# One gathered tile in 64 moved from GpSimd's queue to SyncE's, in a relational graph layer on one core

## The chip, the cores and the metric

The kernel runs on one core of a Trainium2 chip. The time is the device time of one launch, in microseconds. Three runs of the kernel before took 2102.25, 2105.05 and 2107.07 us, with a median of 2105.05 us. The profiled execution is a fourth run and has its own time, which is given below. The engines are named as in the profile: PE is TensorE (PEld its weight loads), DVE is VectorE, ACT is ScalarE, POOL is GpSimd and SP is SyncE. An engine's name with a q behind it (SPq, DVEq) is its sequencer, which issues DMAs, waits for semaphores and loads registers.

## The reference

There are 12,500 nodes with 256 features, and 212,500 edges sorted by destination. Each edge has one of 8 types, and each node's last edge is its loop to itself.

```python
h = jnp.maximum(_layernorm(x, axis=-1), 0.0)
hx = jnp.einsum('ni,rio->rno', h, weight)          # 8 products per node
msg = hx[edge_type, src]
agg = jax.ops.segment_sum(msg, dst, num_segments=num_nodes)
out = x + agg * 0.5 ** 0.5 + h_bias + (h @ loop_weight) * 0.5 ** 0.5
```

## The kernel before

**What is summed where.** The kernel does not form `hx`. It sums the rows of `h` by destination node and edge type first, and multiplies by the 8 weights afterwards. The sums stand transposed in SBUF in `acc`, a ring of 6 slots of 128 nodes.

**Edges.** They are cut into 802 units of 256 edges (in the first 128 units) or 267 edges (after those). A self loop is taken out of a unit's list and handled by node, so what is left fits 256 places. A unit is two tiles of 128 edges, and there are 1603 tiles in all. Units are prepared in 7 blocks of up to 128. For each block `load_indices` (line 304) loads source, destination and type of its edges into `nat_s`, `nat_d` and `nat_t`, some 45 small VectorE steps turn them into row numbers `gidx`, columns `col` and ring offsets, and `blocks_ahead` spreads these steps over the tiles before the block is needed, three steps in every second tile. The last block is not full. There the unused places are filled first: `nat_s` and `nat_t` by a VectorE memset, `nat_d` by a GpSimd iota (line 317). Only then are its rows loaded.

**One tile.** `gather` (line 671) lets GpSimd fetch 128 rows of 256 numbers, chosen by one column of `gidx`, with one indirect DMA (line 683) into `msg`. Until the normalized table `h32` has been written, the rows come from `x` and are normalized in place. After that they come from `h32`. `edge_sums` (line 713) multiplies the rows with a one-hot matrix `oh` in four matmuls (line 723), and `add_sums` (line 731) lets VectorE add the result of a pair of tiles to the ring, at an offset that VectorE's sequencer holds in a register. `load_offsets` (line 704) fills 16 such registers at a time with one load.

**The loop.** It stands in an order written out by hand (line 1030): in step `t` the gather of tile `t + AHEAD` (58) is issued, then the one-hots, the sums of tile `t`, background steps, and pieces of the work on finished groups of 128 nodes. The pool of `msg` has `MSGS // PAIR` = 31 buffers of two tiles. A gather into a buffer waits until the matmuls that read it last are done, so gathers can lead the matmuls by at most about 60 tiles. Each engine takes its own instructions strictly in this order.

**Groups.** When all edges of a group are in, 18 products (line 883) are queued between the following tiles. Three tiles behind them comes `finish` (line 891): VectorE adds `x`, SyncE stores four groups at once (line 900), and the slot is cleared for a later group by `begin` (line 765), which fills it with that group's self loops in eight VectorE instructions (line 773). For these, the loops' types are needed by node. Every fourth group, `finish` calls `mark` (line 780, VectorE), `find_types` (line 793: small TensorE products at line 800 that read what `mark` wrote, then VectorE, then ScalarE) and, three tiles later, `spread_types` (line 822). The order in `finish` is `begin`, `mark`, `find_types`, so in TensorE's list the products of line 800 stand directly behind work on VectorE that is still to be done.

**SyncE** issues all plain transfers, in the order of the loop: the block loads (lines 322 and 325), the loads of `h` and `x` for four groups (line 839) and the stores (line 900). The compiler hands these transfers eight semaphores in turn, and a transfer waits until the one issued eight before it has landed.

Of the kernel before, what the change touches and what calls it, by code (L numbers as in the profile page):

```python
# [11 lines left out]
I32 = mybir.dt.int32  # L12
AF = mybir.ActivationFunctionType
ALU = mybir.AluOpType
# [4 lines left out]
DVE = mybir.EngineType.DVE  # L19

P = 128
EPS = 1e-5
ALPHA = 0.5

# [4 lines left out]
EDGES = 267  # L29
# [9 lines left out]
CLEARED = 3  # L39
RING = GROUP * SLOTS  # L40

MSGS = 62
AHEAD = 58


# [7 lines left out]
REST = 3  # L53
# [2 lines left out]

ROWS = 6
FIRST = 4

LATE = 8  # L60

# [148 lines left out]
def kernel(  # L210
# [11 lines left out]
    nc = tc.nc  # L222
    N, D = x.shape
# [7 lines left out]
    NT = plan.NT  # L231
    U = PAIR * P
    NU = plan.NU
    EU = plan.EU
# [30 lines left out]
    def place_of(t):  # L265
        u, i = divmod(t, PAIR)
        return u // P, i, u % P


    with ExitStack() as main:  # L270
# [25 lines left out]

        outs = [ps_o.tile([P, 2, D], F32, name=f"po{i}") for i in range(2)]
        msg, oh, offsets, kind = {}, {}, {}, {}
        firsts, stops, loops, marked, typed, gidx, col = {}, {}, {}, {}, {}, {}, {}
        added, zeroed = {}, {}  # L300
        state = {"h32": None}
# [2 lines left out]
        def load_indices(b):  # L304

            rows_ = min(P, NU - b * P)
            last = b == NB - 1
            full = rows_ - last
            size = EDGES if b else U
            e0 = P * U + (b - 1) * P * EDGES if b else 0  # L310
            nat = {}
            for name, a, more in (("s", src, 0), ("d", dst, 1 if b else 0), ("t", etype, 0)):
                n = ep.tile([P, EDGES + 1], I32, name=f"nat_{name}")
                if last:

                    if more:
                        nc.gpsimd.iota(
                            n, pattern=[[2, EDGES + 1]], base=N - 2 * EU, channel_multiplier=0)
                    else:
                        nc.vector.memset(n, -1 if name == "d" else 0)  # L320
                if full:
                    nc.sync.dma_start(n[:full, : size + more], bass.AP(
                        tensor=a.tensor, offset=a.offset + e0, ap=[[size, full], [1, size + more]]))
                if last:
                    nc.sync.dma_start(
                        n[full : full + 1, :EU], a[E - EU : E].rearrange("(p q) -> p q", p=1))
                nat[name] = n
            return nat

        def turned(got, cols, to):  # L330

            def turn():
                pt = ps_d.tile([P, 512], F32, tag="pt", name="ptr")
                for i in range(PAIR):
                    half = slice(i * P, (i + 1) * P)
                    nc.tensor.transpose(pt[:, half], got[cols][:, half], ident)
                nc.vector.tensor_copy(to(), pt[:, :U])

            return [turn]
# [5 lines left out]
        def compacted(got, bit, bits):  # L345

            def step(k):
                m = work_tile(got, "moves", 5, I32)
                nc.vector.tensor_single_scalar(m, packed, 1 << (bit + k), op=ALU.bitwise_and)  # L349
                nc.vector.copy_predicated(  # L350
                    packed[:, : EDGES - (1 << k)], m[:, 1 << k :], packed[:, 1 << k :])

            return [lambda k=k: step(k) for k in range(bits)]

        def sources(b, got):


            if b == 0:
                def copy():
                    nc.vector.tensor_copy(work_tile(got, "sf", 2)[:, :U], got["s"][:, :U])  # L360

                return [copy, *turned(
                    got, "sf", lambda: gidx.setdefault(b, idx.tile([P, U], I32, name="gidx")))]

            def rises():
                nc.vector.tensor_tensor(  # L366
                    work_tile(got, "rise", 0), got["d"][:, 1:], got["d"][:, :EDGES], op=ALU.subtract)

            def stays():
                nc.vector.tensor_scalar(  # L370
                    work_tile(got, "stay", 1), got["rise"], 0.0, None, op0=ALU.is_equal)
                firsts[b] = small.tile([P, 1], F32, name="firsts")
                nc.vector.tensor_copy(firsts[b], got["d"][:, 0:1])

            def shifts():
                nc.vector.scalar_tensor_tensor(
                    work_tile(got, "code", 2), got["d"][:, :EDGES], firsts[b], got["stay"],
                    op0=ALU.subtract, op1=ALU.mult)

            def codes():  # L380
                nc.vector.scalar_tensor_tensor(
                    got["code"], got["code"], float(R), got["t"][:, :EDGES], op0=ALU.mult, op1=ALU.add)

            def packs():
                nc.vector.scalar_tensor_tensor(
                    packed, got["s"][:, :EDGES], float(1 << (TB + SB)), got["code"],
                    op0=ALU.mult, op1=ALU.add)

            def unpacks():
                nc.vector.tensor_single_scalar(  # L390
                    work_tile(got, "from", 5, I32)[:, :U], packed[:, :U], TB + SB,
                    op=ALU.logical_shift_right)
                nc.vector.tensor_scalar(
                    work_tile(got, "sf", 2)[:, :U], got["from"][:, :U], 0.0, float(N - 1),
                    op0=ALU.max, op1=ALU.min)
                nc.vector.tensor_single_scalar(
                    work_tile(got, "rest", 3, I32)[:, :U], packed[:, :U], (1 << (TB + SB)) - 1,
                    op=ALU.bitwise_and)

            return [rises, stays, shifts, codes, packs, *compacted(got, TB, SB), unpacks,  # L400
                    *turned(got, "sf", lambda: gidx.setdefault(b, idx.tile([P, U], I32, name="gidx")))]

        def last_edges(b, got):

# [266 lines left out]
        def gather(t):  # L671
            if t % PAIR == 0:
                both = msgs.tile([P, PAIR, D], F32, name="msg")
                for i in range(PAIR):
                    msg[t + i] = both[:, i, :]
            if t % QUAD:
                kind[t] = kind[t - 1]
            else:
                kind[t] = "h" if state["h32"] is not None and t >= state["h32"] + LATE else "x"
            table = {"h": h32, "x": x}[kind[t]]  # L680
            b, i, u = place_of(t)
            at = i * P + u
            nc.gpsimd.indirect_dma_start(  # L683
                out=msg[t], out_offset=None, in_=table[:, :],
                in_offset=bass.IndirectOffsetOnAxis(ap=gidx[b][:, at : at + 1], axis=0))

        def onehots(t):

# [133 lines left out]
        def spread_types(q):  # L822

            pt = ps_d.tile([P, 512], F32, tag="pt", name="ptt")
            nc.tensor.matmul(pt, ones_b, marked.pop(q), start=True, stop=True)
            typed[q] = types.tile([P, XG * GROUP], BF16, name="types")
            nc.scalar.activation(typed[q], pt, AF.Copy)

        got = {}
# [40 lines left out]
        def group_work(g):  # L870
# [20 lines left out]
            def finish():  # L891
                q, k = divmod(g, XG)
                rows_ = got["x", q]
                nc.vector.tensor_add(rows_[:n, k, :], rows_[:n, k, :], outs[g % 2][:n, 1, :])  # L894
                nc.vector.tensor_add(rows_[:n, k, :], rows_[:n, k, :], got["out", g][:n])  # L895
                if XG * (q + 1) >= plan.NG:
                    nc.sync.dma_start(out[d0 : d0 + n], rows_[:n, k, :])
                elif k == XG - 1:
                    first = plan.starts[XG * q]
                    nc.sync.dma_start(  # L900
                        out[first : d0 + n].rearrange("(k p) d -> p k d", p=P), rows_)
                b = g + SLOTS
                q, k = divmod(b, XG)
                if b < plan.NG:
                    if q < plan.typed:
                        clear(b)
                    else:
                        begin(b)
                if q + 1 >= plan.typed and XG * (q + 1) < plan.NG:
                    if k == XG // 4:  # L910
                        load_groups("h", h32, q + 1)
                    if k == XG - 2:
                        mark(q + 1)
                    if k == XG - 1:
                        find_types(q + 1)
                        done["late"].append((done["tile"] + REST, lambda: spread_types(q + 1)))

            def last():
                done["late"].append((done["tile"] + REST, finish))
# [8 lines left out]
        with tc.manual_schedule():  # L928
# [101 lines left out]
            for t in range(NT):  # L1030
                done["tile"] = t
                if t + AHEAD < NT:
                    gather(t + AHEAD)
                blocks_ahead(t)
                for f in after:
                    f()
# [92 lines left out]
```

## Time and profile before

| | |
|---|---|
| median of three runs | 2105.05 us |
| profiled execution: its time, its span | 2107.2 us, 2105.2 us |
| PE busy | 1789.1 us (85%) |
| DVE busy | 1327.7 us (63%) |
| POOL busy | 1523.2 us (72%) |
| gathers (line 683) | 1603 in all: 96 from `x`, 1507 from `h32` |
| granted PE clock, mean | 0.924 |
| DMA | 281.17 MB, mean 134 GB/s |

The span is the profiled stretch from the first instruction to the last. The busy time of an engine is what its instructions took; waits and the sequencer's own work (register loads, DMA issues) are not in it. So an engine that is 72% busy can still be the one that never rests, when there is a fixed gap behind each of its instructions. In the lists of waits, the name behind the arrow is what ended the wait; "issue" means that nothing in the profile ended it.

### The profile page before, as it was taken

Reading aid. Unit: us, or ns where it says so; the run is one execution under the profiler, and the core shown is the slowest. Engines: PE = TensorE matmul, PEld = TensorE weight load, DVE = VectorE, ACT = ScalarE, POOL = GpSimd, SP = SyncE. Lnnn points to the kernel's source line nnn. Section 1 sums busy time; section 2 is a strip of 40 time slices with the busy share of each in tenths; the row PEclk is TensorE's granted clock in tenths of the full one; section 3 lists DMA queues with packets and bytes.
Section 4 is the critical chain, followed back from the end, with each engine's and each line's share of the span. In section 5 each row is a group of like instructions: output and inputs, shape, how many; then the busy total and the mean of one; then the engine's idle time right before and its main releaser. Section 6 shows DMA issues by size and latency. Waiting matters only on the chain.

```text
span 2105.2 us, 29382 instructions
## 1 busy us (share of the span) xinstructions
PE 1789.1 (85%) x10411; PEld 1644.1 (78%) x10411; DVE 1327.7 (63%) x3274; ACT 218.5 (10%) x470; POOL 1523.2 (72%) x1630
## 2 busy tenths in 40 slices
PE   2468999998999998999988998988998860799998
PEld 2357998888898888888877887877888750698897
DVE  7869666668666687665686655577665520856652
ACT  7854100000000000000000000000000000000000
POOL 7767777777777777777777777777777777677750
PEclk8578999998999999999999999999999985899999
DMA  8963443443444344344344344343443433343430
GB/s 297 373 208 103 145 136 106 136 144 106 135 136 135 105 142 135 106 135 136 106 143 131 109 135 135 107 143 106 135 135 106 135 106 106 117 127 105 130 91 15
DMA packets 146904, 281.17 MB, mean 134 GB/s; under 512 B 28125, under 2 KB 95460, under 8 KB 146756
## 3 DMA queue, kind: packets, MB, share of 16 engines
q0 software_dynamic: 76944, 210.21, 34.2%
q1 hardware_dynamic: 69812, 69.05, 10.2%
q8 instruction: 85, 1.39, 0.3%
q14 instruction: 63, 0.52, 0.1%
HBM read 253.55 MB, written 25.60 MB: 133 GB/s over the span
## 4 chain that ended last, share of the span: by engine, by line
PE 67%; DVE 13%; issue 6%; DMA 6%; POOL 4%; ACT 2%; SPq 0%; DVEq 0%; ACTq 0%; POOLq 0%
PE ps L723 34%; PE po L883 31%; DMA msg<-h,gidx 4%; POOL msg L683 4%; DVE acc L773 3%; DVE acc L735 2%; DVE moves L349 2%; DVE fixed L350 2%; DMA h<-xt 1%; ACT xt L645 1%; DVE oh L696 1%; PE pst L759 1%; DMA w<-in_L_gnn_weight_dram 1%; DVE n_stats L633 0%; PE ptt L800 0%
## 5 line engine op out<-in xcount | busy, mean ns | idle before, releaser
L683 POOL DMA_INDIRECT msg<-h,gidx x1507 | 1430.0, 949 | 481.7 <-issue 396.3
L723 PE MATMUL ps<-oh,msg 128*128 128x176 f32 (+1 forms) x6412 | 1146.2, 310 | 187.5 <-DVE acc L735 76.6
L723 PEld LDWEIGHTS ps<-oh,msg 128*128 128x128 f32 x6412 | 1056.2, 198 | 290.1 <-issue 100.9
L883 PE MATMUL po<-w,acc 128*128 128x256 f32 x3136 | 892.7, 387 | 0.0
L696 DVE TENSOR_TENSOR oh<-fixed,cols 128x704 f32<-128x704 f32 x402 | 356.0, 886 | 356.2 <-PE ps L723 349.3
L883 PEld LDWEIGHTS po<-w,acc 128*128 128x128 f32 x3136 | 547.4, 195 | 25.3
L735 DVE TENSOR_TENSOR acc<-acc,ps 128x352 f32 x802 | 412.9, 515 | 180.9 <-PE ps L723 171.9
L773 DVE SCALAR_TENSOR_TENSOR acc<-types,pst 128x256 f32<-128x256 bf16 (+1 forms) x688 | 234.8, 414 | 74.5 <-ACT self_t L762 73.0
L762 ACT ACTIVATE self_t<-pst 128x256 f32<-128x256 f32 x98 | 37.5, 383 | 1524.5 <-PE pst L759 1524.5
L883 PE MATMUL po<-wl,self_t 128*128 128x256 f32 x392 | 121.2, 438 | 3.9 <-ACT self_t L762 2.4
L683 POOL DMA_INDIRECT msg<-in_x_dram,gidx x96 | 90.9, 947 | 31.1 <-issue 26.2
L883 PEld LDWEIGHTS po<-wl,self_t 128*128 128x128 f32 x392 | 75.7, 214 | 11.9 <-ACT self_t L762 2.8
L800 PE MATMUL ptt<-loops,mark 128*128 128x24 bf16 x216 | 9.3, 179 | 80.8 <-DVE acc L773 80.8
L800 PEld LDWEIGHTS <-mark 128*128 128x128 bf16 x216 | 7.3, 101 | 85.7 <-DVE acc L773 85.7
L366 DVE TENSOR_TENSOR rise<-nat_d 128x267 f32<-128x267 int32 x6 | 2.6, 432 | 79.0 <-DMA nat_d<-in_dst_dram 79.0
L645 ACT ACTIVATE xt<-xt,n_shift,n_rstd 128x256 f32<-128x256 f32 x98 | 50.9, 589 | 11.0 <-DVE n_shift L642 11.0
L645 ACT ACTIVATE msg<-msg,e_shift,e_rstd 128x256 f32<-128x256 f32 x96 | 49.6, 589 | 8.5 <-DVE e_shift L642 8.1
L894 DVE TENSOR_TENSOR xr<-xr,po 128x256 f32<-128x256 f32 x98 | 40.4, 412 | 7.4 <-PE po L883 7.4
L895 DVE TENSOR_TENSOR xr<-xr,po 128x256 f32<-128x256 f32 x98 | 41.2, 421 | 3.4
L818 ACT ACTIVATE diagonal<-ident,kinds 128x128 bf16<-128x128 f32 x88 | 28.1, 390 | 113.8 <-DVE kinds L815 113.8
L759 PE MATMUL pst<-ident,hr 128*128 128x128 f32 x196 | 37.7, 274 | 0.4 <-DVE offs L586 0.2
L349 DVE TENSOR_SCALAR moves<-fixed 128x267 int32<-128x267 int32 x84 | 36.4, 433 | 1.7
(200 smaller groups left out, 402.3 us busy)
## 6 DMA issues: line engine op xcount, KB each, us to landing
msg<-h,gidx POOLq DMA_INDIRECT x1507, 2.8
xt<-in_x_dram SPq DMA_DIRECT2D x24, 512.0 KB, 6.4
h<-xt SPq DMA_DIRECT2D x24, 512.0 KB
xr<-in_x_dram SPq DMA_DIRECT2D x24, 512.0 KB, 7.1
hr<-h SPq DMA_DIRECT2D x24, 512.0 KB, 6.3
out_dram<-xr SPq DMA_DIRECT2D x24, 512.0 KB, 4.0
w<-in_L_gnn_weight_dram SPq DMA_DIRECT2D x2, 1024.0 KB, 8.3
msg<-in_x_dram,gidx POOLq DMA_INDIRECT x96, 5.8
```

Source lines behind the costliest of these rows:

```text
L349: nc.vector.tensor_single_scalar(m, packed, 1 << (bit + k), op=ALU.bitwise_and)
L350: nc.vector.copy_predicated(packed[:, : EDGES - (1 << k)], m[:, 1 << k :], packed[:, 1 << k :])
L645: nc.scalar.activation(rows_[j], rows_[j], AF.Relu, bias=shift[:n, j : j + 1], scale=rstd[:n, j : j + 1])
L683: nc.gpsimd.indirect_dma_start(out=msg[t], out_offset=None, in_=table[:, :], in_offset=bass.IndirectOffsetOnAxis(ap=gidx[b][:, at : at + 1 ...
L696: nc.vector.tensor_tensor(o[:, k : k + v, :i, :], iota_f.unsqueeze(1).unsqueeze(1).to_broadcast([P, v, i, C]), of.unsqueeze(3).to_broadcas ...
L723: nc.tensor.matmul(ps[:, c, from_ : from_ + width], m[:, c * P : (c + 1) * P], o[:, :width], start=(i == 0 and c == 0), stop=(end and c == ...
L735: i = nc.vector.tensor_tensor(a, a, ps, op=ALU.add)
L759: nc.tensor.transpose(pst[:, c, :n], rows_[:n, c * P : (c + 1) * P], ident[:n, :n])
L773: i = nc.vector.scalar_tensor_tensor(acc[:, :, r, s0 : s0 + n], of, float(r + 1), pst[:, :, :n], op0=ALU.is_equal, op1=ALU.mult)
L883: i = nc.tensor.matmul(got["out", g][:n], lhs, rhs, start=(r == R and c == 0), stop=(r == R - 1 and c == KC - 1))
L894: nc.vector.tensor_add(rows_[:n, k, :], rows_[:n, k, :], outs[g % 2][:n, 1, :])
L895: nc.vector.tensor_add(rows_[:n, k, :], rows_[:n, k, :], got["out", g][:n])
```

## The change

There are four edits.

- **Rows fetched by SyncE.** In blocks 1 to 6, a tile whose number is 63 modulo 64 is no longer gathered by GpSimd (if it lies within the loop's reach and `h32` is in use). Its 128 rows are fetched by 128 single-row DMAs on SyncE's queue. The row numbers come from a new tile `single` (an integer copy of the second half of the block's row numbers, not transposed): a register load brings 16 of them to SyncE, and 16 DMAs follow, each from an address computed from its register. `fetch(FETCH)` puts three of these items (a load or a DMA) into each step of the loop. There are 20 such tiles, 319 to 1535, so 2560 DMAs, 160 register loads and 2560 address computations are added to SyncE's list, and 20 gathers leave GpSimd's.
- **`MSGS` 60 instead of 62**: one buffer of two tiles less, `AHEAD` unchanged.
- **The last block's places** of `nat_d` are filled by VectorE from `line`, not by GpSimd's iota.
- **`find_types` three tiles later**, and `spread_types` three tiles after that.

```diff
@@ constants
-MSGS = 62
+MSGS = 60
 AHEAD = 58
+SINGLE = 64
+FETCH = 3
+SOURCES = 16
@@ load_indices
                     if more:
-                        nc.gpsimd.iota(
-                            n, pattern=[[2, EDGES + 1]], base=N - 2 * EU, channel_multiplier=0)
+                        nc.vector.tensor_scalar(
+                            n, line[:, : EDGES + 1], 2.0, float(N - 2 * EU), op0=ALU.mult, op1=ALU.add)
@@ new: the last step of sources(b, got)
+        def kept_sources(b, got):
+            def keep():
+                single[b] = idx.tile([P, P], I32, name="single")
+                nc.vector.tensor_copy(single[b], got["sf"][:, P:U])
+            return [] if b == 0 else [keep]
@@ gather
             b, i, u = place_of(t)
+            if b and i and kind[t] == "h" and t % SINGLE == SINGLE - 1 and t + AHEAD < NT:
+                for r in range(0, P, SOURCES):
+                    fetches.append(lambda r=r: load_sources(t, r))
+                return
             at = i * P + u
             nc.gpsimd.indirect_dma_start(
@@ new
+        def load_sources(t, r0):
+            b, _, u = place_of(t)
+            _, vals = nc.values_load_multi_w_load_instructions(
+                single[b][u : u + 1, r0 : r0 + SOURCES], engines=[SP], min_val=0, max_val=N - 1,
+                skip_runtime_bounds_check_because="clamped to the table where they are computed")
+            for i, v in reversed(list(enumerate(vals))):
+                fetches.insert(0, lambda i=i, v=v: nc.sync.dma_start(
+                    msg[t][r0 + i : r0 + i + 1, :], h32[bass.ds(v, 1), :]))
+        def fetch(n):
+            for _ in range(min(n, len(fetches))):
+                fetches.pop(0)()
@@ finish
                     if k == XG - 1:
-                        find_types(q + 1)
-                        done["late"].append((done["tile"] + REST, lambda: spread_types(q + 1)))
+                        done["late"].append((done["tile"] + REST, lambda: find_types(q + 1)))
+                        done["late"].append((done["tile"] + 2 * REST, lambda: spread_types(q + 1)))
@@ loop
                 if t + AHEAD < NT:
                     gather(t + AHEAD)
+                fetch(FETCH)
                 blocks_ahead(t)
```

More of the change, by code (lines that the diff above doesn't have):

```diff
@@ L21 @@
 P = 128
+SP = mybir.EngineType.SP
 EPS = 1e-5
@@ L298 @@
         msg, oh, offsets, kind = {}, {}, {}, {}
+        single, fetches = {}, []
         firsts, stops, loops, marked, typed, gidx, col = {}, {}, {}, {}, {}, {}, {}
@@ L400, in sources @@
             return [rises, stays, shifts, codes, packs, *compacted(got, TB, SB), unpacks,
-                    *turned(got, "sf", lambda: gidx.setdefault(b, idx.tile([P, U], I32, name="gidx")))]
+                    *turned(got, "sf", lambda: gidx.setdefault(b, idx.tile([P, U], I32, name="gidx"))),
+                    *kept_sources(b, got)]
         def last_edges(b, got):
```

## The prediction, made before the changed kernel ran

> **What bounds the kernel now.** I read the costliest groups first, then the waits, then windows by stage. The chain of waits is read last: it ends in TensorE, and it hides what set the pace.
>
> ```profile
> PE 67%; DVE 13%; issue 6%; DMA 6%; POOL 4%; ACT 2%; SPq 0%; DVEq 0%; ACTq 0%; POOLq 0%
> L683 POOL DMA_INDIRECT msg<-h,gidx x1507 | 1430.0, 949 | 481.7 <-issue 396.3
> ...
> POOL msg L683 <- issue: 306.8, 1007, 0.3
> POOL msg L683 <- PE ps L723: 31.4, 103, 0.3
> ...
> PE ps L723 <- DMA msg<-h,gidx: 25.7, 37, 2.0
> ```
>
> The second line is the key. A gather takes 0.949 us, and most of the idle time before gathers is "issue", which nothing ended. The two POOL waits are those between 225 and 1710 us: none is longer than 0.3 us. So GpSimd starts a gather every 1.25 us (0.95 and a fixed 0.30) and is full at 72% busy. The last line is TensorE from 975 to 1710 us: it waits for gathered rows 37 times, so the rows set the pace there. The windows (start and end, length, busy time and number, for TensorE its weight loads beside it, then granted clock, DMA share, GB/s) count gathers in the first three lines and tile matmuls, four a tile, in the last two:
>
> ```profile
> 125.00:225.00 100.00, 68.55 (x73) 0.85 0.42 125
> 225.00:975.00 750.00, 567.84 (x599) 0.96 0.44 128
> 975.00:1710.00 735.00, 556.49 (x587) 0.96 0.43 126
> ...
> 225.00:975.00 750.00, 451.14 (x2612) 422.85 (x2610) 0.96 0.44 128
> 975.00:1710.00 735.00, 418.36 (x2350) 378.62 (x2351) 0.96 0.43 126
> ```
>
> GpSimd holds 750/599 = 735/587 = 1.252 us per gather. TensorE does 653 tiles in the first long window, 1.149 us each, and eats its backlog (58 tiles at 225 us, 4 at 975 us by counting both). After that it goes at GpSimd's pace. From 125 to 225 us there are 73 gathers where 80 would fit: the `msg` buffers are full there.
>
> Then something else happens:
>
> ```profile
> DVE rise L366 <- DMA nat_d<-in_dst_dram: 79.0, 2, 74.4
> PE ptt L800 <- DVE acc L773: 80.8, 21, 7.8
> PE ps L723 <- DVE acc L735: 76.6, 11, 66.6
> ...
> 1782.61 0.37 POOL L317 IOTA nat_d<- 128x268 int32 x1
> ...
> 1784.86 0.44 DVE L366 TENSOR_TENSOR rise<-nat_d 128x267 f32<-128x267 int32 x1 [74.36 <-DMA nat_d<-in_dst_dram]
> ...
> 1787.02 1.51 PE L723 MATMUL ps<-oh,msg 128*128 128x176 f32 x4 [66.64 <-DVE acc L735]
> ```
>
> The iota of the last block takes 0.37 us, but in GpSimd's list it stands behind the 58 gathers that the loop issues ahead. VectorE waits 74.4 us for the load behind it, and TensorE 66.6 us for VectorE. GpSimd goes on gathering, fills its buffers, and is then held by TensorE. At its last gather (2035.8 us) TensorE still has some 40 tiles to do, so the stall comes back as a late end: the span is 2105.2 us.
>
> **Part by part.**
>
> *Iota moved to VectorE.* It removes the 74.4 us wait, and with it TensorE's 66.6 us. Late next is GpSimd's own pace: TensorE stays 4 tiles behind the gathers to the end. The fill itself costs VectorE about 0.44 us (L366 above, nearly the same shape). VectorE now waits for its loads, which stand in SyncE's list behind 11 rows of a fetch: 11 x 0.41 (below) + 6 loads x 0.35 + landing 1.8 (1783.00, the load's issue, to 1784.86) is about 8 us instead of 74, and the chain of gathers does not see it.
>
> *20 gathers leave GpSimd.* 20 x 1.252 = 25 us off the chain that sets the pace.
>
> *One `msg` pair less.* Where the buffers are full (before 225 us), gathers lead by two tiles less: 2 x 1.25 = 2.5 us later from there on.
>
> *Type products three tiles later.* They take up to 80.8 us of waits from TensorE. TensorE is ahead of its rows or catching up with them, so I count nothing. What hides it is the gather pace; with that cover gone it would be worth up to 80 us. The residual wait is bounded by today's 3.8 us per call; the latest user of the types comes 10 tiles after `spread_types`.
>
> *The sum for GpSimd's chain.* By 224.7 us 168 gathers have started (96 from `x`, 72 from `h32`). Of 1603, 1435 are left; plus 2, less 20, is 1417. Tile 1600 is the third from the end: 224.7 + 1414 x 1.252 = 1995, and 2.8 us to landing (page, part 6) gives 1998. The end is the same program as now:
>
> ```profile
> 2080.66 0.76 PE L723 MATMUL ps<-oh,msg 128*128 128x176 f32 x4
> ```
>
> That is tile 1600, 24.5 us before the span's end (the queued products of the last groups). 1998 + 24.5 = 2022.5 us of span. The execution is 2.0 us longer than its span, and the median of the runs lies 2.15 us below the profiled one: 2022.
>
> *The 2560 row fetches.* This is the price that no row shows. Per tile, SyncE needs 128 x (address, DMA, two gaps) and 8 loads of 16 registers. The nearest rows:
>
> ```profile
> L325 SPq DMA_DIRECT2D nat_d<-in_dst_dram x1: 233/233/233, 1783.4 to 1783.4; - x1
> L325 SPq DMA_DIRECT2D nat_t<-in_edge_type_dram x1: 246/246/246, 1784.0 to 1784.0; - x1
> ...
> L735 DVEq FUSED_REGOPS  x802: 69/69/69, 39.6 to 2086.3; - x161
> L602 SPq FUSED_REGOPS  x1: 181/181/181, 1831.7 to 1831.7; - x1
> L707 DVEq TENSOR_LOAD <-offs x51: 539/1100/3781, 12.2 to 2042.5; - x51
> ```
>
> L325 loads a single row: 0.246 us of SyncE, from a fixed address; a register's address may cost more. The address is between 0.07 (VectorE's sequencer, also multiplications for an address) and 0.18 (SyncE's own, but comparisons). I take 0.07, the same kind of work. The gaps are 0.045 each (SyncE's loads at 1710.24 and 1710.60, the first taking 0.32). So a row is 0.41 us (0.52 with the other end), 128 rows 52 us, the loads 8 x 1.15 = 9.2: 61 us. Between the rows stand a store, a load of `h` and one of `x` (0.38, 0.50, 1.07 by their medians, 2.1 with gaps), and as a transfer waits for the one eight before it, the 512 KB loads (6.3 and 7.1 us to landing) hold the rows for up to 3.0 and 3.8 us. The fetch of a tile takes 61 to 70 us. The time it has: its first row waits for the matmuls 60 tiles earlier, and 60 tiles at the new pace (1.252 x 63/64 = 1.232) are 74 us, less 2.1 for landing (the shortest load on the page is an estimate for it): 72. It fits, with 2 to 11 us to spare. I add 6 us for loads that collide and rows that come late: **2028 us**.
>
> [...]
>
> **The rivals.**
>
> *SyncE becomes the bound (slower).* If a fetch takes F > 72 us, TensorE waits for its last row, and gathers, at most 60 tiles ahead, wait with it: each of some 18 to 20 cycles is longer by F - 72. Back at today's time when the excess is (2105 - 2022)/19 = 4.4 us, that is F = 76 us or a row of about 0.47 us. With the upper address price (0.52 us) F is 76 to 85, and the time 2022 + 19 x (4 to 13) = 2098 to 2270; middle 2165. For it: the margin is thin, and the register address is unpriced. Against: the one-row DMAs are short, and SyncE has little else to do, a store and two loads per 65 tiles.
>
> *SyncE late by little.* Rows of 0.44 to 0.47 us: 2040 to 2095.
>
> *TensorE becomes the bound.* At 1.149 us per tile from tile 110 (225 us) it would do tile 1600 at 1937 us, 60 before the rows. It would have to lose 4% first; if the wait of the last block came back in full at the same place, the end would be about 2022 + 58 = 2080.
>
> *The removed gathers or the iota bring nothing.* Without the 20 gathers' gain the sum is 2047. GpSimd's row shows no slack in which it could vanish.
>
> **How the numbers follow.** Chances: the forecast 0.52; SyncE late by little 0.07; SyncE the bound and slower 0.37; about equal 0.02; the two others 0.02. Forecast's own range: 2015 to 2045 (chain sum less 7 for a better start, plus 23 for some late cycles). The range for 8 in 10 goes up into SyncE's case, to 2200 (rows of 0.52 us in the middle of their stalls), and down to 2012. A measurement of this kernel tells 0.2% from no change (4 us; its three runs lie within 0.23%). Faster 0.60, same 0.02, slower 0.38.
>
> **What would show it.** Right: no wait of 66 us in TensorE; gathers 1.25 us apart to the end, the last near 1998 us; SyncE's rows at most 0.43 us apart; no wait of TensorE for rows fetched by SyncE above 1 or 2 us. L800's waits shrink without moving the end. Wrong: TensorE waiting every 64 tiles for `msg` landing from SyncE, and gathers waiting for TensorE behind it; then the row's price was the failed step. A start of a fetch held by a store's wait would be another.

## The result and the profile after

The changed kernel takes 2031.35 us (median of six runs) where the kernel before takes 2105.78 us: a ratio of 0.9641, with a 95% interval of 0.9627 to 0.9654. The forecast was 2028 us. One of the six executions took 3686.84 us; it has no profile, the ratio leaves it out (without it the median is 2030.82 us), and nothing here explains it. The profiled execution is 2030.82 us, its span 2029.1 us.

The page of the changed kernel, the chain that ended last by engine and the gathers' group:

```profile
PE 33%; SPq 24%; issue 14%; DMA 11%; DVE 11%; POOL 4%; ACT 2%; DVEq 0%; ACTq 0%; POOLq 0%
...
L703 POOL DMA_INDIRECT msg<-h,gidx x1487 | 1411.4, 949 | 467.8 <-issue 387.2
```

20 gathers fewer, at the same 949 ns. The chain now names SyncE with 24%, though its rows turn out below to cost almost nothing; in the equally fast run without the moved types (below) it names SyncE with 10%. So a share in this view is no price: where two causes end nearly together, it names the later one.

Windows of the changed kernel, gathers (start and end, length, busy time and number, granted clock, DMA share, GB/s):

```profile
125.00:225.00 100.00, 64.67 (x69) 0.83 0.41 121
225.00:975.00 750.00, 567.78 (x599) 0.97 0.45 130
975.00:1710.00 735.00, 556.34 (x587) 0.97 0.44 129
1710.00:2000.00 290.00, 219.62 (x232) 0.99 0.42 121
```

GpSimd starts as many gathers per stretch as before (599 and 587), and goes on like that to the end: 290/232 = 1.25 us. That is the pace of the whole kernel. Only the first window is worse, 69 gathers where the kernel before has 73. From 225 us on nothing holds GpSimd: of all its waits there, none is longer than the fixed 0.3 us (in all, times, longest, us):

```profile
POOL msg L703 <- issue: 365.7, 1200, 0.3
POOL msg L703 <- PE ps L757: 40.2, 132, 0.3
```

Windows of the changed kernel, tile matmuls of TensorE and their weight loads, four of each a tile:

```profile
225.00:975.00 750.00, 456.96 (x2640) 426.82 (x2640) 0.97 0.45 130
975.00:1710.00 735.00, 424.33 (x2380) 380.30 (x2379) 0.97 0.44 129
```

TensorE does 660 tiles in the first and 595 in the second: 7 or 8 more than before in each. The rows that SyncE brings come on top of the same number of gathers.

The waits of the changed kernel over the whole run:

```profile
POOL msg L703 <- PE ps L757: 44.7, 139, 2.6
PE ps L757 <- DMA msg<-h,gidx: 38.0, 60, 2.6
...
PE ps L757 <- DMA msg<-h: 30.4, 8, 6.1
...
DVE rise L381 <- DMA nat_d<-in_dst_dram: 22.6, 4, 6.9
...
PE ptt L834 <- DVE acc L807: 4.2, 2, 3.3
```

The wait of 74.4 us of VectorE and that of 66.6 us of TensorE are gone; the longest wait for a block's load is 6.9 us. The types' waits (line 834, which was 800) fell from 80.8 to 4.2 us. New is the third line: 8 times TensorE waits for rows that SyncE fetched.

SyncE's rows in the changed kernel, by instruction (ns: least, median, most), and in three stretches that hold one fetch each:

```profile
L710 SPq TENSOR_LOAD <-single x160: 1182/1282/2922, 368.9 to 1907.6; - x160
...
L714 SPq FUSED_REGOPS  x2560: 37/37/51, 371.9 to 1915.2; - x197
L714 SPq MOVE msg<-h x2560: 29/29/38, 382.5 to 1915.2; - x197
L714 SPq DMA_DIRECT2D msg<-h x2560: 224/225/940, 382.6 to 1915.3; - x197
...
L714 SPq DMA_DIRECT2D msg<-h x128: 224/225/307, 382.6 to 445.9; - x128
L714 SPq DMA_DIRECT2D msg<-h x128: 224/225/940, 1295.8 to 1364.2; - x128
L714 SPq DMA_DIRECT2D msg<-h x128: 224/225/758, 1690.7 to 1762.1; - x128
```

A row is an address (37 ns), a move (29 ns) and a DMA (225 ns); with the gaps, rows are 0.41 us apart (median). The last three lines give 63.3, 68.4 and 71.4 us from the first row to the last; all 20 fetches lie between 63 and 71 us.

The timeline of the changed kernel (start, length, engine, line, operation; in brackets the idle time before it), first the last block's fill, then tile 1600:

```profile
1693.82 0.24 DVE L324 TENSOR_SCALAR nat_d<-line 128x268 int32<-128x268 f32 x1
1697.90 0.44 DVE L381 TENSOR_TENSOR rise<-nat_d 128x267 f32<-128x267 int32 x1 [3.56 <-DMA nat_d<-in_dst_dram]
...
2004.20 0.83 PE L757 MATMUL ps<-oh,msg 128*128 128x176 f32 x4 [0.43 <-DMA msg<-h,gidx]
```

The fill costs 0.24 us, and the first user of the last block's rows comes 4 us later, after a wait of 3.56 us. Tile 1600 starts at 2004.2 us, 24.9 us before the end, with a wait for a gather: GpSimd sets the end.

### The profile page after: what moved, and what is told of

Its sections match the earlier page's. It is cut to its first block, busy times and chain, and to the rows that moved or that the text cites. A ratio compares the mean times of both kernels' runs of the same rounds, so it can differ in the third digit from the quotient of the medians.

```text
span 2029.1 us, 37425 instructions
## 1 busy us (share of the span) xinstructions
PE 1784.7 (88%) x10411; PEld 1627.0 (80%) x10411; DVE 1324.2 (65%) x3281; ACT 218.4 (11%) x470; POOL 1504.2 (74%) x1609
## 4 chain that ended last, share of the span: by engine, by line
PE 33%; SPq 24%; issue 14%; DMA 11%; DVE 11%; POOL 4%; ACT 2%; DVEq 0%; ACTq 0%; POOLq 0%
SPq L714 19%; PE ps L757 17%; PE po L917 15%; DMA msg<-h,gidx 5%; SPq L710 5%; POOL msg L703 4%; DVE acc L769 2%; DMA xr<-in_x_dram 1%; DVE moves L356 1%; DVE fixed L357 1%; DMA h<-xt 1%; DVE oh L730 1%; DMA hr<-h 1%; DVE acc L807 1%; DMA msg<-h 1%
## 5 line engine op out<-in xcount | busy, mean ns | idle before, releaser
L703 POOL DMA_INDIRECT msg<-h,gidx x1487 | 1411.4, 949 | 467.8 <-issue 387.2
L807 DVE SCALAR_TENSOR_TENSOR acc<-types,pst 128x256 f32<-128x256 bf16 (+1 forms) x688 | 234.9, 414 | 95.5 <-ACT self_t L796 94.4
L917 PE MATMUL po<-wl,self_t 128*128 128x256 f32 x392 | 106.6, 396 | 3.9 <-ACT self_t L796 2.4
L917 PEld LDWEIGHTS po<-wl,self_t 128*128 128x128 f32 x392 | 70.0, 199 | 10.3 <-ACT self_t L796 2.8
L357 DVE COPY_PREDICATED fixed<-moves,fixed 128x266 int32<-128x266 int32 (+6 forms) x84 | 33.7, 401 | 2.9
L649 DVE BATCH_NORM_STATS2 n_stats<-xt 128x6 f32<-128x256 f32 x98 | 34.4, 411 | 0.9 <-issue 0.7
L343 PE MATMUL ptr<-ident,sf 128*128 128x128 f32 x14 | 4.5, 421 | 33.5 <-DVE sf L408 30.2
```

What stands on the lines that cost most here:

```text
L357: nc.vector.copy_predicated(packed[:, : EDGES - (1 << k)], m[:, 1 << k :], packed[:, 1 << k :])
L703: nc.gpsimd.indirect_dma_start(out=msg[t], out_offset=None, in_=table[:, :], in_offset=bass.IndirectOffsetOnAxis(ap=gidx[b][:, at : at + 1 ...
L807: i = nc.vector.scalar_tensor_tensor(acc[:, :, r, s0 : s0 + n], of, float(r + 1), pst[:, :, :n], op0=ALU.is_equal, op1=ALU.mult)
L917: i = nc.tensor.matmul(got["out", g][:n], lhs, rhs, start=(r == R and c == 0), stop=(r == R - 1 and c == KC - 1))
```

## The experiments

The theory: GpSimd's gathers set the pace, the last block's stall and 20 gathers are what is saved, and SyncE's fetch fits in its time with little to spare. Its rival: SyncE's rows are, or are close to being, the bound. Each ratio is against the kernel before on the same chip (2105.9 us for the first four runs, 2106.7 us for the next four, which were on a second chip). Where runs of these two chips are compared with each other or with the changed kernel's 2031.35 us, it is across chips on which the kernel before agrees within 1 us.

**One part alone, and one part undone.** First the fill alone, on the kernel before:

```diff
-nc.gpsimd.iota(n, pattern=[[2, EDGES + 1]], base=N - 2 * EU, channel_multiplier=0)
+nc.vector.tensor_scalar(n, line[:, : EDGES + 1], 2.0, float(N - 2 * EU), op0=ALU.mult, op1=ALU.add)
```

> The kernel before with one edit: VectorE fills the last block's places. If GpSimd's chain of gathers sets the pace (my theory), the 66 us stall of TensorE goes and nothing else: the changed kernel's 2031 plus 25 us for the 20 gathers that are back, less about 5 us for the four gathers that the smaller buffer pool cost, 2051 us, with the last gather about 24 us before the end. If the stall was hidden by the gathers anyway (rival), the time stays at 2105.

Measured: 2048.75 us, ratio 0.9727 (0.9711 to 0.9743). Waits of this kernel:

```profile
PE ptt L800 <- DVE acc L773: 80.8, 21, 7.8
...
PE ps L723 <- DMA msg<-h,gidx: 39.5, 53, 2.8
...
DVE rise L366 <- DMA nat_d<-in_dst_dram: 7.5, 2, 4.2
```

57 us come from moving one instruction of 0.37 us out of a list in which it stood behind 58 others. The types' waits are all still there, 80.8 us, and TensorE still waits for gathers 53 times, so it has time to spare.

Next the rows with one `msg` pair less, without the other two edits:

```diff
-MSGS = 62
+MSGS = 60
+SINGLE = 64
...             # and all of load_sources, fetch, kept_sources
```

> The kernel before with the row fetches and the smaller pool; the iota stays on GpSimd, find_types where it was. Theory: the iota stands behind 18 gathers less, so it comes about 18 us earlier (1765 instead of 1783), TensorE stalls all the same, and what follows the stall is as long as before: 2105 - 18 = 2087. Rival (a shorter chain of gathers is worth its full 25 us less 5): 2085, not to be told apart by the time, but then without a stall. Rival (the rows of SyncE cost TensorE time): above 2105.

Measured: 2092.27 us, 0.993 (0.9914 to 0.9947), 5 us above the 2087 expected. The iota comes 19.7 us earlier than before, and the stall stays, as its waits show:

```profile
1762.92 0.38 POOL L324 IOTA nat_d<- 128x268 int32 x1
...
DVE rise L381 <- DMA nat_d<-in_dst_dram: 89.1, 5, 69.8
...
PE ps L757 <- issue: 77.5, 10, 64.6
```

With the stall in place, TensorE's backlog behind it sets the end, and 20 gathers fewer are worth 13.6 us. Without it they are worth 21.2 us (2048.75 to 2027.55, next but one run).

Next the types' products alone, on the kernel before:

```diff
-find_types(q + 1)
-done["late"].append((done["tile"] + REST, lambda: spread_types(q + 1)))
+done["late"].append((done["tile"] + REST, lambda: find_types(q + 1)))
+done["late"].append((done["tile"] + 2 * REST, lambda: spread_types(q + 1)))
```

> The kernel before with find_types three tiles later only. Theory: up to the stall the gathers hide it; after the stall TensorE is alone the bound for some 245 tiles, with four calls of 3.8 us each: 2105 - 15 = 2090. Rival (TensorE is the bound throughout): 2105 - 77 = 2028. Rival (moved waits come back elsewhere): 2105.

Measured: 2090.15 us, 0.9924 (0.9908 to 0.9941). In the kernel before, TensorE sets the end after the stall; there the types' waits count. The profile of before has 9.9 us of them after 1787 us, and the profile of this run has none there. That is the larger part of the 15.8 us. The mean granted clock between 1787 and 2092 us is also a little higher, 0.96 against 0.94; whether that is the rest was not tested.

Then the same edit undone in the changed kernel (the diff above, reversed).

> The changed kernel with find_types back where it was. Theory: the gathers hide the 80 us of waits in TensorE: 2031, at most 5 more. Rival (TensorE, which now also waits for SyncE's rows, has no room left): each of 21 calls costs its 3.8 us, up to 2110.

Measured: 2027.55 us, 0.9627 (0.9611 to 0.9643), where the changed kernel has 0.9641 (0.9627 to 0.9654). Its waits:

```profile
POOL msg L703 <- issue: 418.5, 1352, 5.7
...
PE ptt L834 <- DVE acc L807: 81.6, 21, 8.6
```

81.6 us of TensorE's waits come back and the time does not move (the two intervals overlap). So the edit is worth 15.8 us in a kernel whose end TensorE sets, and nothing in one where the gathers leave TensorE that much time. They leave it just that much: in this trace TensorE never waits for a gather (60 times in the changed kernel), and tile 1600 comes at the end without a wait before it:

```profile
2004.98 0.76 PE L757 MATMUL ps<-oh,msg 128*128 128x176 f32 x4
```

So here TensorE and GpSimd end together, and with fewer gathers still the types' waits would count again. The gain of the whole change is about 57 us for the fill, 21 us for the gathers (with the lost pair), nothing for the types.

**How much room SyncE has.** Loads of 4 registers, so that a fetch takes longer:

```diff
-SOURCES = 16
+SOURCES = 4
```

> The changed kernel with four row numbers per register load instead of 16: 32 loads per tile instead of 8. A load of 16 took 1.28 us on SyncE and a load of one 0.47 us, so one of four about 0.63: a tile's fetch gets 11 us longer, 74 to 82 us instead of 63 to 71. By my limit of 72 us per fetch and 18 to 20 cycles the time is 2031 + 19 x 5 = about 2125, between 2070 and 2180, and gathers wait for TensorE. Rival (the rows have more room than I counted): 2031.

Measured: 2181.67 us, 1.0356 (1.0338 to 1.0373), just above the expected range. SyncE's loads and two fetches of this kernel:

```profile
L710 SPq TENSOR_LOAD <-single x640: 477/568/1752, 366.8 to 2077.7; - x160
...
L714 SPq DMA_DIRECT2D msg<-h x128: 224/225/295, 1062.0 to 1136.3; - x128
L714 SPq DMA_DIRECT2D msg<-h x128: 224/228/295, 1144.1 to 1219.8; - x128
```

and its waits:

```profile
PE ps L757 <- DMA msg<-h: 229.0, 17, 17.0
...
POOL msg L703 <- PE ps L757: 128.4, 135, 7.5
```

The fetch is 74 to 82 us here, some 11 us longer, and the kernel is 150 us longer, 7.5 us for each of 20 fetches. TensorE waits for SyncE and GpSimd for TensorE: this is the rival that ends slower. Fetches start 85.4 us apart (median) and take 76 (median), so some 9.4 us of each cycle lie outside the fetch (landing, 1.2 to 1.9 us for a fetch's last row in the changed kernel's trace, and waiting for the buffer; 6.4 to 12.6 over the cycles). At the pace of the gathers a cycle is 63 x 1.254 = 79 us, so by this estimate the limit of a fetch is about 69.6 us. A second estimate agrees: fetches that are 11.3 us longer (75.9 against 64.6 by their medians) cost 7.5 us each, so 3.8 us were free, a limit of 68.4. The changed kernel's fetches, 63 to 71, reach it: the median one has some 4 or 5 us to spare, the longest none.

Half as many rows:

```diff
-SINGLE = 64
+SINGLE = 128
```

> The changed kernel with one tile in 128 fetched by rows. Theory: ten gathers are back on GpSimd, 12.5 us more, 2043 us. Rival (SyncE's rows cost TensorE time): 2031 or less.

Measured: 2041.49 us, 0.9691 (0.9673 to 0.9708). Ten gathers more cost 10.1 us. By the pace it would be 12.5, so the other ten tiles' 1280 rows cost about 2.4 us, which the intervals do not tell from nothing.

**A second queue.** Every second run of 16 rows on ScalarE's queue, three items a step on each:

```diff
+k = r // SOURCES % 2
...
-engines=[SP]
+engines=[(SP, ACT)[k]]
...
-nc.sync.dma_start(
+(nc.sync, nc.scalar)[k].dma_start(
```

> The changed kernel with every second run of 16 rows fetched by ScalarE's queue instead of SyncE's: a fetch takes about half, 32 to 36 us, and TensorE no longer waits for rows. Theory: the gathers set the pace, no gain, 2026 to 2033. Rival (the 24% of the chain of waits that stand at SyncE, and the 30 us that TensorE waits for its rows, are time on the path): 2000 to 2010. If ScalarE's own work suffers by it: above 2040.

Measured: 2094.5 us, 0.9943 (0.9925 to 0.9961), 63 us more than the changed kernel, so the theory's "no gain" and the rival's gain both failed, and the third case came true. The timeline of this kernel has both queues side by side (count of rows at the end):

```profile
1020.88 12.99 SPq L716 DMA_DIRECT2D msg<-h  x24
1020.88 13.33 ACTq L716 DMA_DIRECT2D msg<-h  x26
```

and its waits:

```profile
ACT self_t L799 <- DMA msg<-h: 703.2, 31, 30.5
...
DVE acc L810 <- ACT self_t L799: 210.0, 52, 13.2
```

But 26 rows take ScalarE 13.33 us, 0.51 each with the register loads between them, and three items are put into a step of 1.25 us, so ScalarE falls behind the loop. The copies that VectorE and TensorE need (line 799) stand behind rows: VectorE waits up to 13.2 us for them and 210.0 us in all, where the changed kernel has 6.9 and 94.4. Beside this, SyncE's rows now wait for the landing of other rows, 179 times, up to 3.5 us, of which the changed kernel's trace shows none. How the 63 us divide between the two was not tested.

One tile in 32, on SyncE and ScalarE in turn:

```diff
-SINGLE = 64
+SINGLE = 32
+k = t // SINGLE % 2
...              # the other lines as above
```

> One tile in 32 fetched by rows, in turn by SyncE and by ScalarE, so that each queue has one tile in 64 as SyncE has now. 40 tiles instead of 20 leave GpSimd's list. Theory: 20 x 1.25 = 25 us less, 2006 us; TensorE's own pace would allow 1965. Rival (TensorE or ScalarE is then the bound: 128 issues of 0.41 us per 64 tiles stand ahead of ScalarE's copies for TensorE): 2025 to 2060.

Measured: 2402.98 us, 1.1397 (1.137 to 1.1424), far above both cases. Waits of this kernel:

```profile
DVE acc L810 <- ACT self_t L799: 421.7, 64, 15.8
...
POOL msg L705 <- PE ps L760: 355.5, 166, 12.7
...
PE ptt L837 <- DVE acc L810: 135.4, 19, 11.8
```

The same waits, larger: 20 more gathers are removed, but VectorE waits for ScalarE's copies for 421.7 us and GpSimd is held by TensorE for 355.5 us. SyncE's rows wait for landings here too (289 times, up to 15.4 us), so it is not ScalarE alone that is shown to be late. In both runs, an engine whose compute others wait for was no free queue.

**The last four runs were on another chip, where the kernel before is slower.** It takes 2578.26 us there (median of 23 runs, 2562.87 to 2592.5). Whether that is the chip or its condition at that time is not known. The expectations were written in times of the other chips and don't apply as numbers; the comparisons within the chip do. They were a quarter of the rows on ScalarE at one item a step, the same with one tile in 48, the fill with the smaller buffers alone, and the changed kernel once more:

```diff
+k = int(r % 64 == 48)                          # a quarter of the rows on ScalarE
+for f, n in zip(fetches, (n, 1)): ...          # three items a step on SyncE, one on ScalarE
```

> The changed kernel with 32 of the 128 rows of a fetched tile on ScalarE's queue, put into the order at one item per step (SyncE keeps 96 rows at three per step). A row took ScalarE 0.38 to 0.55 us and a step is 1.25 us, so ScalarE's own copies are held by half a microsecond and not by 13. Theory (the gathers set the pace; what cost 63 us when both queues had three items per step was ScalarE's backlog): 2026 to 2034, with a fetch of about 50 us on SyncE. Rival (rows on ScalarE's queue cost as such): a quarter of the 256 ScalarE rows' price or more, above 2045.

Measured: 2570.36 us, 0.9974 (0.9947 to 1.0001).

```diff
-SINGLE = 64
+SINGLE = 48                                    # and the two lines above
```

> The same with one tile in 48 instead of 64. Six or seven more gathers leave GpSimd's list, 26 or 27 instead of 20: 6.5 x 1.25 = 8 us less than the changed kernel, 2023. The fetch of 50 us has 48 x 1.23 = 59 us less about 9 between two fetches, so it just fits. Rival (it does not fit, or TensorE has no room left): 2031 to 2080.

Measured: 2890.9 us, 1.1219 (1.1178 to 1.126). Waits of this kernel:

```profile
POOL msg L705 <- PE ps L760: 407.6, 148, 30.6
...
PE ps L760 <- DMA msg<-h: 284.9, 19, 24.2
```

A fetch every 48 tiles does not fit on this chip, though SyncE has a quarter less to do in each: TensorE waits for its rows up to 24.2 us.

```diff
-MSGS = 62
+MSGS = 60                                      # on the kernel before, with the fill on VectorE
```

> The kernel before with VectorE's fill and the smaller buffer pool, no row fetches. Against the fill alone (2048.75) it prices the missing pair of buffers. Prediction's step: 2.5 us, 2051. By the four gathers that the changed kernel's trace is short of at 225 us: 5 us, 2054. Together with the 20 gathers at 1.25 us it must come to the changed kernel's 2031 plus 25, 2056.

Measured: 2576.29 us, 0.9996 (0.9969 to 1.0023).

The changed kernel, with no edit:

> The changed kernel once more, on the same chip as the others of this call: 2026 to 2033. It tells whether the kernel without the moved type products (2027.55) is really as fast.

Measured: 2732.11 us, **1.0608** (1.057 to 1.0647). On this chip the change makes the kernel slower. Windows of the tile matmuls from 700 to 1500 us, first the fill alone on the first chip:

```profile
700.00:1500.00 800.00, 453.93 (x2577) 414.46 (x2577) 0.96 0.43 126
```

then the fill with the smaller buffers on this chip:

```profile
700.00:1500.00 800.00, 389.79 (x2092) 353.64 (x2091) 0.89 0.35 103
```

and the changed kernel on this chip:

```profile
700.00:1500.00 800.00, 368.56 (x1954) 335.93 (x1952) 0.87 0.33 97
```

A tile takes 800/(2577/4) = 1.24, 1.53 and 1.64 us. One matmul is only 6% longer in the second than in the first (186 against 176 ns busy, at a lower granted clock, 0.89 against 0.96); the rest lies between the instructions. In the waits of the fill with the smaller buffers on this chip it is called "issue", which nothing in the profile ended:

```profile
PEld ps L723 <- issue: 275.8, 246, 48.3
POOL msg L683 <- PE ps L723: 259.1, 122, 8.6
...
PE ps L723 <- issue: 170.8, 169, 31.7
```

(46.3 and 8.5 us in the two "issue" rows of the fill alone on the first chip.) GpSimd is held by TensorE for 259.1 us there, against 45.3: TensorE sets the pace, and the fill together with the smaller buffers brings nothing. That no stall stood at the iota in the kernel before on this chip was not seen, since there is no profile of it.

The changed kernel on this chip, SyncE's rows over the whole run, the address first:

```profile
L714 SPq FUSED_REGOPS  x2560: 2/37/1422, 497.5 to 2628.5; - x197
L714 SPq DMA_DIRECT2D msg<-h x2560: 2/225/1124, 518.1 to 2628.6; - x197
```

and its waits:

```profile
POOL msg L703 <- PE ps L757: 409.1, 177, 13.9
...
PE ps L757 <- DMA msg<-h: 296.3, 20, 19.9
```

The medians of the DMA (225 ns) and of the address (37 ns) are those of the first chip, but single ones take up to 1.1 and 1.4 us, rows are 0.66 us apart (median) and a fetch takes 93 to 101 us. SyncE's rows also wait for the landing of earlier rows here, 136 times and 56.8 us in all; the trace on the first chip shows none of these waits. TensorE waits for SyncE's rows 20 times, up to 19.9 us. The arithmetic of the limit holds here too, as an estimate: 64 tiles x 1.53 = 98 us, less 9.4, is a limit of 88.6; a fetch of 97 exceeds it by 8.4, 20 of them by 168 us, and 2732.11 - 2576.29 = 156 was measured (with the types moved as well, whose worth on this chip is not known). With a quarter of the rows on ScalarE, 162 us come back (2732.11 to 2570.36). So the rival mechanism is real, and only its threshold kept it out on the first chips. What makes the instructions of this chip uneven and further apart stays open.

## Why the prediction was right

- **The mechanism.** GpSimd's list of gathers sets the end; the fill takes the stall out; the next thing late is GpSimd itself. All three hold: 1.254 us a gather (1.252 taken), no wait of GpSimd above 0.3 us from 225 us on, and 3.56 us of wait for the last block's load (8 taken; 6.9 is the longest of any block).
- **The sum.** Tile 1600 was put at 1998 us and came at 2004.2. The pace, 1.254 us and not 1.252 over 1414 gathers, is 2.8 us of it. By 225 us 165 gathers had started, where the kernel before has 169 and the sum took off 2 for the pair: 2.5 us. How much of that the lost pair costs is not shown, since the run with the rows alone, which has the same pool, had started 168. The last landing took 3.8 us and not 2.8: 1.0 us. Last, the median was put just below the span and lies 2.2 us above it. So the 6 us that were added for "loads that collide and rows that come late" came out nearly right as a number, but by luck: other terms filled it, and the rows of ten tiles cost some 2.4 us or nothing.
- **The gathers.** 25 us for the gathers less 2.5 for the pair were taken; 21.2 us were measured.
- **The row's price.** 0.41 us was taken and measured. In its parts, the address is two instructions of 37 and 29 ns (0.07 taken together), the DMA 0.225 (0.246), the gaps 0.12 in all (0.09), a load of 16 registers 1.28 (1.15, VectorE's). So two terms were off by 0.02 and 0.03 us against each other. The open point was what a register's address costs: the DMA took 0.225 us with it, where the two from a fixed address took 0.233 and 0.246. The fetch was put at 61 to 70 us and took 63 to 71. In the changed kernel's trace 19 rows wait for the landing of a load or store issued eight before, up to 2.3 us (3.0 and 3.8 taken).
- **The limit was too high.** 72 us was the limit of a fetch; the estimates from the runs are 68 to 70, and 63 to 71 was the fetch. So the margin was not 2 to 11 us but some 4 or 5, and nothing for the longest. What was counted too low is the time outside the fetch: 9.4 us of a cycle by the run with loads of 4, where 2.1 us for landing and four tiles (60 of 64, 5 us) were counted. Few fetches were late and only by little, so the time did not show it.
- **A sign that was wrong.** "No wait of TensorE for rows fetched by SyncE above 1 or 2 us": there are 8, up to 6.1 us, 30.4 us together. TensorE has the time for them, since the gathers' pace covers it: no gather is held by more than 0.3 us.
- **The types at nothing** was right, and so was the cover named for it: with the cover gone the same edit is worth 15.8 us. But the cover is just thick enough: without the edit TensorE waits for no gather any more.
- **The chance of slower.** 0.37 was given to SyncE as the bound. On the first chips it lost; on the last one it is what happens, for the reason given (rows of over 0.47 us, 0.66 there), at a price of 156 us.

Open are: the price of the lost pair alone; whether a quarter of the rows on ScalarE is a gain on the first chips; how the cost of rows on ScalarE divides; and what slows the last chip. No version was found that beats the changed kernel clearly; the one without the moved types (2027.55 us) is as fast.

## What to carry to other kernels

An engine's list is a queue: price a small instruction by what stands before it in that list (0.37 us of iota were worth 57 us), and judge whether an engine is full by its pace, not by its busy share (GpSimd sets the end at 74% busy). A removed wait counted here only where its engine set the end, so the same edit was worth 16 us in one version and nothing in the other. Where a gain rests on work that fits into a fixed time with a thin margin, as a fetch of 63 to 71 us in about 70, say so with the change: here the same kernel gains 3.6% on one chip and loses 6.1% on another.

## What was not expected of the hardware

- A single-row DMA takes SyncE 0.225 us from a register's address, less than one from a fixed address in the profile of before (0.233 and 0.246, one of each and of 0.2 KB, where the rows have 1 KB); ScalarE's takes 0.213 us (median of the run with a quarter of the rows there, on the last chip).
- A register load on SyncE takes 0.57 us for 4 registers and 1.28 for 16, so by an estimate from these two about 0.06 us a register and 0.33 a load. That share, paid 640 times instead of 160, with the gaps around each load, was enough to make the kernel 150 us longer.
- A chip on which the kernel before takes 2578 us instead of 2106, with a gather of the same length (951 against 949 ns) and the same median for a one-row DMA (225 ns), but with uneven sequencer instructions (an address of 2 to 1422 ns where the first chip has 37 to 51) and rows 0.66 us apart instead of 0.41.
